# One rotation of eight PSUM banks in a sliding-window attention between two feed-forward layers: scores, maxima and sums in a new order

## The chip, the cores and the metric

The kernel runs on one core of a Trainium2 chip. A core has five engines that run side by side and wait for each other through semaphores: PE (TensorE) multiplies matrices, DVE (VectorE) and ACT (ScalarE) work on elements and can read PSUM, POOL (GpSimd) works on elements in SBUF alone, and SP (SyncE) issues DMA transfers. Results of PE land in PSUM, which has eight banks of 128 partitions by 512 fp32 values; before a bank is written again, whoever reads it has to be done. The metric is the device time of one execution in microseconds, the lower the better; the time before is the median of three runs.

## The reference

The input `x` is (8, 512, 512): eight rows of 512 tokens with 512 features. A feed-forward layer, an attention and the same feed-forward layer again are added to it:

```python
x = x + 0.5 * _L0_ffn_ref(_layernorm(x), w_gate_up, w_proj)
x = x + _L0_attn_ref(_layernorm(x), Wq, Wk, Wv, Wo)
x = x + 0.5 * _L0_ffn_ref(_layernorm(x), w_gate_up, w_proj)
```

The feed-forward layer quantises its weights to three values per group of 64, and computes `silu(gate) * up`, an RMS norm and a projection. The attention has 32 heads of 16 features and a window of 128 tokens:

```python
q, k, v = heads(x @ Wq.T), heads(x @ Wk.T), heads(x @ Wv.T)
kw, vw = ...   # each block of 128 queries sees its own and the previous block of keys
scores = jnp.einsum('bhnrd,bhncd->bhnrc', qb, kw) * scale
valid = (dist >= 0) & (dist <= window) & (key_global >= 0)
probs = jax.nn.softmax(jnp.where(valid, scores, min), axis=-1)
out = jnp.einsum('bhnrc,bhncd->bhnrd', probs, vw) ... @ Wo.T
```

## The kernel before

There are three stages: feed-forward a (`ffn_stage("a")`), attention (`attention_stage`) and feed-forward c. The change is in the attention and in the first row of stage c, which begins while the attention's last row still runs (class `FirstRow`, lines 610 to 690).

The attention is cut into 128 units: 8 rows b, in each 4 groups j of eight heads, in each 4 blocks t of 128 queries; unit u = (4b + j) * 4 + t, and i = u // 4 numbers the groups. A loop over u (line 1052) writes down the order of all engines' instructions by hand: inside `manual_schedule` (line 1041) each engine executes its instructions in the order of the program, so an instruction that waits holds up everything behind it on its engine. Waits are found by the framework: an instruction waits for the writers of what it reads, and for the last reader of a bank or buffer that it takes over.

In one step of the loop PE gets, in this order:

- `probabilities(u)` (line 917), "sp": the transposed scores of the unit, 24 matmuls of 32 rows each into four banks (three parts: two for the scores, one that adds the negated maxima `ms`). Each bank is read by a Relu: banks 0, 2 and 3 on ACT (L944), bank 1 on DVE (L940). Then ACT takes the exponential of all four (L946), and POOL clears what lies outside the window (L951, one or two instructions). The result is `pT`.
- `weighted(u - 1)` (line 957), "av": the weighted sums of the unit before, 32 matmuls (16 where t is 0) of 32 columns. Two units share one bank of the pool `ps_av`, and every second unit ACT copies it to `sums` (L977).
- `maxima(u + 6)` (line 873), "sm": the scores of the unit six steps ahead, 16 matmuls into four banks, for the maxima alone. DVE reads each bank twice (L892, eight instructions that add the window and reduce).
- every fourth unit `maxima_turned`, "neg": the maxima transposed (L911); DVE splits them in two terms just before (L902, L903).
- one projection (L808, four matmuls of 128x512), which one depends on t: at t = 0 `values` ("wv"), at t = 1 the output of an earlier row ("wo", from the second row on), at t = 2 `queries` ("wq"), at t = 3 `keys` ("wk"). Queries and keys are split into a high and a low term by `two_terms` (line 819): ACT writes the high term (L821), DVE the difference (L822); SP then moves them to `qs` and `ks` (L839, L851), which are used from three units later on. Values are copied by DVE in two halves (L864). The output is added to the residual by DVE (L1030).
- in four units of each row a transpose of the next row's normed tokens, "ptn_b" (L227), copied by ACT (L235).

The eight banks are divided: `ps_s` (line 757) has six, which the score tiles, neg and the transposes take in turn; `ps_av` and `ps_mm` have one each, for the sums and for projections. Before the first unit, steps of the loop with negative u make the first queries, keys, values and maxima. In the last row (u from 116 on) the place of the projection is taken by a chunk of stage c's first row: `row_c.chunk` (line 653), 16 matmuls into two banks, a Silu on ACT and a product on DVE; from `down_at` on, `row_c.down` makes its down projection.

Of the kernel before, what the change touches and what calls it, by code (L numbers as in the profile page):

```python
# [8 lines left out]
F32 = mybir.dt.float32  # L9
# [3 lines left out]
ALU = mybir.AluOpType  # L13
AX = mybir.AxisListType

P = 128
# [8 lines left out]
def macaron_block(  # L25
# [19 lines left out]
    nc = tc.nc  # L45
    B, T, D = x.shape
# [47 lines left out]
    PSUM = bass.MemoryType.PSUM  # L94
# [147 lines left out]
    def ffn_stage(kind, source, target, first):  # L242
# [18 lines left out]
        def banks_opened():  # L261
            for name, bufs in (("tr", 2), ("acc", 4), ("mm", 2)):
                banks[name] = pool(s, f"ps_{name}_{kind}", bufs, PSUM), name
            banks["ms"] = banks["mm"]

        def bank(use, shape, name):
            space, tag = banks[use]
            return space.tile(shape, F32, tag=tag, name=name)
# [21 lines left out]
                True, f"{kind}{b}", each=first and b == 1,  # L290
            )

        def gate_or_up(b, c, i, use="mm"):
            ps = bank(use, [P, T], f"gu_{kind}{b}_{c}_{i}")
# [315 lines left out]
        class FirstRow:  # L610
# [1 line left out]

            KEPT = 2

            def opened(self, ps_s, ps_av, ps_mm, xpool, xn, terms):
                nonlocal xnpool
                banks["mm"] = banks["acc"] = banks["tr"] = ps_s, "s"
                banks["ms"] = ps_mm, "mm"
                self.ps_av = ps_av
                xspools.append(terms)  # L620
                xpools.append(xpool)
                xnpool = xn
                self.kept, self.terms = {}, {}
                row_loaded(0)
                self.norm = norms[0]
                self.coming = []
# [9 lines left out]
            def load(self):  # L636
                if self.coming:
                    weights_loaded([self.coming.pop(0)])

            def down_opened(self):  # L640
                nonlocal hpool
                hpool = pool(s, f"h_{kind}", 3, side="right")
                xpools.append(pool(s, f"x1_{kind}", 1, side="right"))
                projection_made(pool(s, f"weights_p_{kind}", 1, side="right"))
                n = (FC - self.KEPT) // 2
                self.coming_down = [*range(n, FC // 2), *range(n)]
# [6 lines left out]
            def chunk(self, c, use):  # L653
                if c == 0:
                    self.sumsq = work.tile([P, T], F32, tag="ss", name=f"ss_{kind}0", bufs=1)
                gate = gate_or_up(0, c, 0, use)
# [15 lines left out]
            def down(self, n):  # L672
                order = [*range(FC - self.KEPT, FC), *range(FC - self.KEPT)]
                if n == 0:
                    self.ops = outputs(0)
                    banks["tr"] = self.ps_av, "av"
# [22 lines left out]

        def rest():  # L700
            xspools.append(2 * [pool(s, f"xs1_{kind}", 2)])
            banks_opened()
            for b in range(1, B):
                row(b)
            s.close()
# [20 lines left out]
    def attention_stage(row_c):  # L726
# [27 lines left out]
        fixed["wq"] = pool(asked, "wq_b", 1)  # L754

        s = ExitStack()
        ps_s = pool(s, "ps_s", 6, PSUM)
        ps_av = pool(s, "ps_av", 1, PSUM)
        ps_mm = pool(s, "ps_mm_b", 1, PSUM)

        xss, norms = {0: begun["norm"][0]}, {}

# [31 lines left out]
            nc.gpsimd.memset(tile_.bitcast(F32), 0.0)  # L794

        xrs = {}
        qs, ks, ms, pTs, avs, sums, dens_sb, reps, oTs = {}, {}, {}, {}, {}, {}, {}, {}, {}
        NJ = DC
        units = B * NJ * TB

# [1 line left out]
            return u // TB // NJ, u // TB % NJ, u % TB  # L802

        def sum_of_products(name, pairs, done):
            space, tag = (ps_mm, "mm") if 0 <= u < units else (ps_s, "s")
            ps = space.tile([P, T], F32, tag=tag, name=name)
            for n, (lhs, rhs) in enumerate(pairs):
                nc.tensor.matmul(ps, lhs, rhs, start=(n == 0), stop=(n == len(pairs) - 1))  # L808
            done(ps)
# [8 lines left out]

        def two_terms(name, ps, by):
            kept = raw.tile([P, 2, T], F32R, tag=name[0], name=name)  # L820
            nc.scalar.activation(kept[:, 0, :], ps, AF.Copy, scale=by)  # L821
            nc.vector.scalar_tensor_tensor(  # L822
                kept[:, 1, :], ps, by, kept[:, 0, :].bitcast(F32), ALU.mult, ALU.subtract
            )
            return kept

# [28 lines left out]
        def values(b, t):  # L855
            rows = slice(t * P, (t + 1) * P)
            pairs = [(xss[b][0][:, k, rows], attn_w["wv"][:, k, :]) for k in range(DC)]


            def kept(ps):  # L860
                heads = vones[b % 2][:, t].rearrange("p (j h g) d -> p h j g d", h=2, g=NG)
                made = ps.rearrange("p (j h g d) -> p h j g d", h=2, g=NG, d=DK)
                for h in range(2):
                    nc.vector.tensor_copy(heads[:, h, :, :, h::2], made[:, h])  # L864

            sum_of_products(f"wv_{b}_{t}", pairs, kept)

# [89 lines left out]
        def weighted(u):  # L957

            i, t = u // TB, u % TB
            b, j = i // NJ, i % NJ  # L960
            if t % 2 == 0:
                avs[i] = ps_av.tile([P, 2, 2, P], F32, tag="av", name=f"av_{u}")
            for h in range(2):
                blocks = [(t - 1, 1), (t, 0)] if t else [(t, 0)]
                for n, (block, m) in enumerate(blocks):
                    for g in range(NG):
                        nc.tensor.matmul(  # L967
                            avs[i][32 * g : 32 * g + 32, h, t % 2, :],
                            vones[b % 2][:, block, NG * (2 * j + h) + g, :],
                            pTs[u - t + block][:, 2 * g + h, m * P : (m + 1) * P],  # L970
                            start=(n == 0), stop=(n == len(blocks) - 1),
                        )

            if t % 2 == 1:
                if t == 1:
                    sums[i] = work.tile([P, 2, T], F32, tag="sums", name=f"sums_{i}", bufs=2)
                nc.scalar.copy(  # L977
                    sums[i][:, :, (t - 1) * P : (t + 1) * P],
                    avs.pop(i).rearrange("p h m q -> p h (m q)"),
                )  # L980

        def rows_of(t, h):

# [68 lines left out]
        for u in range(-3 * TB, down_at + FC):  # L1052
            i, t = u // TB, u % TB
            b, j = i // NJ, i % NJ
            if u == closing - row:
                row_c.opened(ps_s, ps_av, ps_mm, xpool, xnpool, [begun["xs0"], fixed["wv"]])
            if u == closing:
                first_values.close()
                row_c.working()
# [16 lines left out]
            if u == units + 1:  # L1076
                scores.close()
                row_c.weights(range(FC - 1, FC))
                row_c.load()
                row_c.down_opened()  # L1080
            if closing <= u < units:
                row_c.load()
                row_c.load()
            if 0 <= u < units:
                probabilities(u)
            if j == 3 and t == 1 and 1 < b + 3 < B:
                row_loaded(b + 3)
# [51 lines left out]
            if down_at - 3 <= u:  # L1139
                row_c.load_down()  # L1140
            if u in chunk_at:
                row_c.chunk(chunk_at[u], "mm" if u in outputs else "ms")
            if u >= down_at:
                row_c.down(u - down_at)
        row_c.ended()
# [37 lines left out]
```

## Time and profile before

| what | value |
|---|---|
| runs | 2391.74, 2395.63, 2397.71 us; median 2395.63 |
| the profiled execution | 2397.86 us, span 2396.1 us |
| busy over the span | PE 97%, weight loads 72%, DVE 55%, ACT 41%, POOL 38% |
| 0 to 803 us, stage a | PE busy 766.23 us, granted clock 0.99 |
| 803 to 847, before the first unit | PE 41.87 |
| 847 to 999, the first 24 units, most without an output projection | PE 143.94, clock 0.94 |
| 999 to 1565, 88 units, 22 groups | PE 564.50 of 566, DVE 388.37, ACT 342.59, POOL 201.76, clock 1.00 |
| 1565 to 1686, the last row with chunks of stage c | PE 112.16 of 121, clock 0.97 |
| 1686 to 1740, the last outputs and the down projection | PE 52.98 of 54 |
| 1740 to 2396, the rest of stage c | PE 646.57 of 656 |

The span is the time from the first to the last instruction; the execution's own time holds a little more. Rows of the timeline read: start in us, duration, engine, line, operation, tile written and tiles read, shapes, how many are merged, and in brackets how long the engine sat idle before and what ended that. PEld is the loading of a matmul's stationary operand, which can run under the matmul before it. Matmuls overlap each other, so the end of a merged row reaches a little into the next; the step from one start to the next start is what a block costs. Busy time on PE includes short waits inside a row of merged matmuls.

### The profile page before, as it was taken

The page shows a single profiled execution, that of the slowest core. Times are in us where ns is not written, and L with a number is a line of the kernel's source. Part 1 is how long each engine was busy: PE and PEld are TensorE (multiplying, and loading weights), DVE is VectorE, ACT ScalarE, POOL GpSimd, SP SyncE. Part 2 cuts the span into 40 slices and gives each one's busy share as a digit, 9 for nine tenths or more (in the row PEclk, how much of TensorE's full clock was granted, in tenths as well). Part 3 has the DMA queues.
Part 4 walks back from the last instruction along what each step waited for, and adds up shares of the span by engine and source line. Part 5 has one row for each costly group of instructions (what it writes and reads, how often), then busy time and mean ns, then how long its engine had stood idle before and what let it go on. Part 6 is the DMA issues. An engine that isn't in the chain of part 4 may idle for free.

```text
span 2396.1 us, 42976 instructions
## 1 busy us (share of the span) xinstructions
PE 2328.3 (97%) x16824; PEld 1718.5 (72%) x16824; DVE 1308.7 (55%) x3685; ACT 985.1 (41%) x1422; POOL 903.4 (38%) x746
## 2 busy tenths in 40 slices
PE   5999999999999999999999999999999999999998
PEld 4778888888888555555565555566688888888886
DVE  7884544444543566767667676664354444444433
ACT  6773222222222156656666656567322222222221
POOL 0000345445445223333333333335334544544544
PEclk9899999999999999999999999999999999999999
DMA  4443200100100324344444445363610010010000
GB/s 160 147 146 134 90 18 18 36 18 18 36 36 36 105 69 110 90 120 118 116 119 119 115 102 135 98 179 125 217 61 22 15 36 18 18 36 18 18 18 18
DMA packets 90283, 186.30 MB, mean 78 GB/s; under 512 B 22496, under 2 KB 26592, under 8 KB 87008
## 3 DMA queue, kind: packets, MB, share of 16 engines
q1 hardware_dynamic: 74768, 142.40, 21.1%
q10 hardware_dynamic: 15312, 41.16, 4.6%
q8 instruction: 132, 2.16, 0.4%
q14 instruction: 71, 0.58, 0.1%
HBM read 78.91 MB, written 45.88 MB: 52 GB/s over the span
## 4 chain that ended last, share of the span: by engine, by line
PE 91%; DVE 5%; ACT 2%; issue 1%; DMA 1%; POOL 0%; ACTq 0%; POOLq 0%; DVEq 0%
PE gu_c L297 19%; PE gu_a L297 18%; PE o_c L330 10%; PE o_a L330 9%; PE wv L808 5%; PE wo L808 5%; PE wq L808 5%; PE wk L808 5%; PE av L967 4%; PE sp L932 4%; PE sm L884 4%; PE neg L911 1%; PE ptn_a L227 1%; PE ptn_c L227 1%; ACT pT L946 1%
## 5 line engine op out<-in xcount | busy, mean ns | idle before, releaser
L297 PE MATMUL gu_a<-xs_a,wgu_a 128*128 128x512 f32 x2048 | 497.0, 396 | 8.0 <-ACT sg_a L308 3.0
L297 PE MATMUL gu_c<-xs_c,wgu_c 128*128 128x512 f32 x2048 | 495.1, 395 | 0.4 <-ACT sg_c L308 0.4
L297 PEld LDWEIGHTS gu_a<-xs_a,wgu_a 128*128 128x128 f32 x2048 | 385.4, 190 | 91.5 <-ACT sg_a L308 4.3
L951 POOL TENSOR_SCALAR_AFFINE_SELECT pT<-pT 128x1024 f32<-128x1024 f32 x224 | 243.7, 1108 | 533.4 <-ACT pT L946 533.4
L297 PEld LDWEIGHTS gu_c<-xs_c,wgu_c 128*128 128x128 f32 x2048 | 383.7, 189 | 84.1 <-issue 1.8
L892 DVE CUSTOM_DVE_ANT_0 seen<-sm,window 128x256 f32<-128x256 f32 (+1 forms) x1024 | 331.4, 388 | 83.9 <-PE sm L884 83.0
L330 PE MATMUL o_a<-wp_a,hs_a 128*128 128x512 f32 x1024 | 257.1, 396 | 1.5 <-DVE hs_a L322 1.4
L330 PE MATMUL o_c<-wp_c,hs_c 128*128 128x512 f32 x1024 | 254.6, 393 | 0.0
L313 DVE TENSOR_TENSOR h_c<-gu_c,sg_c 128x512 f32<-128x512 f32 x128 | 88.4, 690 | 295.1 <-PE gu_c L297 256.5
L586 POOL TENSOR_TENSOR sq_c<-h_c 128x512 f32<-128x512 f32 x120 | 125.2, 1044 | 298.6 <-DVE h_c L313 287.4
L944 ACT ACTIVATE pT<-sp 128x512 f32<-128x512 f32 x372 | 176.2, 545 | 131.2 <-PE sp L932 131.2
L330 PEld LDWEIGHTS o_a<-wp_a,hs_a 128*128 128x128 f32 x1024 | 192.9, 190 | 41.9 <-DVE hs_a L322 2.3
L330 PEld LDWEIGHTS o_c<-wp_c,hs_c 128*128 128x128 f32 x1024 | 191.9, 188 | 43.0 <-issue 1.9
L946 ACT ACTIVATE pT<-pT 128x2048 f32<-128x2048 f32 (+1 forms) x128 | 217.4, 1698 | 6.9 <-DVE pT L940 2.4
L313 DVE TENSOR_TENSOR h_a<-gu_a,sg_a 128x512 f32<-128x512 f32 x128 | 88.3, 690 | 232.4 <-PE gu_a L297 227.7
L587 POOL TENSOR_TENSOR ss_c<-ss_c,sq_c 128x512 f32<-128x512 f32 x120 | 188.4, 1570 | 9.0
L586 POOL TENSOR_TENSOR sq_a<-h_a 128x512 f32<-128x512 f32 x90 | 94.3, 1048 | 225.1 <-DVE h_a L313 215.6
L308 ACT ACTIVATE sg_c<-gu_c 128x512 f32<-128x512 f32 x128 | 76.7, 599 | 245.7 <-PE gu_c L297 236.0
L318 ACT CAST hs_c<-h_c 128x512 fp32r<-128x512 f32 x114 | 70.8, 621 | 226.1 <-DVE h_c L313 226.1
L308 ACT ACTIVATE sg_a<-gu_a 128x512 f32<-128x512 f32 x128 | 76.4, 597 | 209.0 <-PE gu_a L297 201.7
L318 ACT CAST hs_a<-h_a 128x512 fp32r<-128x512 f32 x115 | 71.3, 620 | 205.0 <-DVE h_a L313 202.6
L322 DVE TENSOR_TENSOR hs_c<-h_c,hs_c 128x512 fp32r<-128x512 f32 x114 | 111.0, 974 | 74.4 <-ACT hs_c L318 74.4
(134 smaller groups left out, 3024.5 us busy)
## 6 DMA issues: line engine op xcount, KB each, us to landing
ks<-k SPq DMA_DIRECT2D x128, 256.0 KB
qs<-q SPq DMA_DIRECT2D x128, 128.0 KB
wf_gu<-w_gate_up_dram SPq DMA_DIRECT2D x16, 512.0 KB
wgu_kept<-wgu_a ACTq DMA_DIRECT2D x16, 512.0 KB
rows_a<-x_a ACTq DMA_DIRECT2D x8, 1024.0 KB
x_b<-rows_a SPq DMA_DIRECT2D x8, 1024.0 KB
oT<-sums SPq DMA_DIRECT2D x64, 128.0 KB
rep<-inverses SPq DMA_DIRECT2D x256, 32.0 KB
```

The source lines that it names most:

```text
L297: nc.tensor.matmul(ps, wgu[c][:, i * DC + k, :], xss[b][part][:, k, :], start=(k == 0 and part == 0), stop=(k == DC - 1 and part == 1),)
L308: nc.scalar.activation(sg, gate, AF.Silu)
L313: nc.vector.tensor_tensor(h, up, sg, ALU.mult)
L318: nc.scalar.copy(hs[:, 0, :], h)
L330: nc.tensor.matmul(ops[t], hs[:, part, t * P : (t + 1) * P], wp[e // 2][:, e % 2, :], start=(e == begin and part == 0), stop=(e == end and ...
L586: nc.gpsimd.tensor_tensor(sq, h, h, ALU.mult)
L587: nc.gpsimd.tensor_tensor(sumsq, sumsq, sq, ALU.add)
L808: nc.tensor.matmul(ps, lhs, rhs, start=(n == 0), stop=(n == len(pairs) - 1))
L892: nc.vector.tensor_tensor_reduce(out=seen[:, : n * P], in0=tiles[g][:, h, : n * P], in1=window[:, (2 - n) * P :], scale=-1.0, scalar=3.4e3 ...
L944: nc.scalar.activation(under, tiles[g][:, :, : n * P], AF.Relu, scale=-1.0)
L946: nc.scalar.activation(seen, seen, AF.Exp, scale=-1.0)
L951: nc.gpsimd.affine_select(out=half, in_=half, compare_op=ALU.is_ge, fill=0.0, base=0, pattern=[[0, 2 * NG], [sign, P]], channel_multiplier ...
```

## The change

Four things, in the attention and its overlap with stage c:

1. Banks. `ps_s` gets all eight banks, and `ps_av` and `ps_mm` are gone: scores, maxima, sums, neg, projections and transposes take banks from one rotation. The sums no longer share a bank between two units: each unit has its own tile and its own copy to `sums`, with half the columns. At `down_at` the pool is closed, and stage c opens its own pools (2, 4 and 2 banks), which it did only after its first row before.
2. Order. `weighted(u - 1)` moves behind `maxima(u + 6)`, and `denominators` with it; neg, when there is one, follows the sums.
3. `two_terms`. DVE no longer subtracts ACT's term: it writes the whole scaled value (`tensor_scalar`, L822), and POOL subtracts ACT's term in place (L823). SP's transfers of the low term follow POOL.
4. `values`. The second half of the copy moves from DVE to ACT (L865).

In the changed file the lines after 822 lie a few further on: L892 becomes L893, L940 to L946 become L941 to L947, L951 becomes L952; the sums' matmuls keep L967, their copy becomes L976, the output's add L1026, and the projections' matmuls become L807.

```diff
-            def opened(self, ps_s, ps_av, ps_mm, xpool, xn, terms):
+            def opened(self, ps_s, xpool, xn, terms):
                 nonlocal xnpool
                 banks["mm"] = banks["acc"] = banks["tr"] = ps_s, "s"
-                banks["ms"] = ps_mm, "mm"
-                self.ps_av = ps_av
+                self.banks = banks
...
+            def own_banks(self):
+                banks_opened()
...
-        ps_s = pool(s, "ps_s", 6, PSUM)
-        ps_av = pool(s, "ps_av", 1, PSUM)
-        ps_mm = pool(s, "ps_mm_b", 1, PSUM)
+        own_banks = ExitStack()
+        ps_s = pool(own_banks, "ps_s", 8, PSUM)
...
         def sum_of_products(name, pairs, done):
-            space, tag = (ps_mm, "mm") if 0 <= u < units else (ps_s, "s")
+            space, tag = (ps_s, "s") if u < down_at else row_c.banks["mm"]
...
             kept = raw.tile([P, 2, T], F32R, tag=name[0], name=name)
+            whole = kept[:, 1, :].bitcast(F32)
             nc.scalar.activation(kept[:, 0, :], ps, AF.Copy, scale=by)
-            nc.vector.scalar_tensor_tensor(
-                kept[:, 1, :], ps, by, kept[:, 0, :].bitcast(F32), ALU.mult, ALU.subtract
+            nc.vector.tensor_scalar(whole, ps, by, None, ALU.mult)
+            nc.gpsimd.tensor_tensor(
+                kept[:, 1, :], whole, kept[:, 0, :].bitcast(F32), ALU.subtract
             )
...
-                for h in range(2):
-                    nc.vector.tensor_copy(heads[:, h, :, :, h::2], made[:, h])
+                nc.vector.tensor_copy(heads[:, 0, :, :, ::2], made[:, 0])
+                nc.scalar.copy(heads[:, 1, :, :, 1::2], made[:, 1])
...
-            if t % 2 == 0:
-                avs[i] = ps_av.tile([P, 2, 2, P], F32, tag="av", name=f"av_{u}")
+            av = ps_s.tile([P, 2, P], F32, tag="s", name=f"av_{u}")
...
-                            avs[i][32 * g : 32 * g + 32, h, t % 2, :],
+                            av[32 * g : 32 * g + 32, h, :],
...
-            if t % 2 == 1:
-                if t == 1:
-                    sums[i] = work.tile([P, 2, T], F32, tag="sums", name=f"sums_{i}", bufs=2)
-                nc.scalar.copy(
-                    sums[i][:, :, (t - 1) * P : (t + 1) * P],
-                    avs.pop(i).rearrange("p h m q -> p h (m q)"),
-                )
+            if t == 0:
+                sums[i] = work.tile([P, 2, T], F32, tag="sums", name=f"sums_{i}", bufs=2)
+            nc.scalar.copy(sums[i][:, :, t * P : (t + 1) * P], av)
...
+            if u == down_at:
+                own_banks.close()
+                row_c.own_banks()
...
-            if 0 <= u - 1 < units:
-                weighted(u - 1)
...
-                if t == 0:
-                    denominators(i - 1)
...
             if 0 <= u + AHEAD < units:
                 maxima(u + AHEAD)
+            if 0 <= u - 1 < units:
+                weighted(u - 1)
+            if t == 0 and 0 <= i - 1 < B * NJ:
+                denominators(i - 1)
```

The rest of the diff drops the argument `use` of `gate_or_up` and `chunk`, the list `avs`, the tag of `ps_av` in `down`, and the opening of stage c's banks in `rest`.

More of the change, by code (lines that the diff above doesn't have):

```diff
@@ L291, in row_loaded, with gate_or_up @@
             )
-        def gate_or_up(b, c, i, use="mm"):
-            ps = bank(use, [P, T], f"gu_{kind}{b}_{c}_{i}")
+        def gate_or_up(b, c, i):
+            ps = bank("mm", [P, T], f"gu_{kind}{b}_{c}_{i}")
             for k in range(DC):
@@ L651, in load_down, with chunk @@
                     nc.sync.dma_start(wp[u].bitcast(F32), wp_kept[u])
-            def chunk(self, c, use):
+            def chunk(self, c):
                 if c == 0:
                     self.sumsq = work.tile([P, T], F32, tag="ss", name=f"ss_{kind}0", bufs=1)
-                gate = gate_or_up(0, c, 0, use)
+                gate = gate_or_up(0, c, 0)
                 up = gate_or_up(0, c, 1)
@@ L675, in down @@
                     self.ops = outputs(0)
-                    banks["tr"] = self.ps_av, "av"
                 if n + 2 < FC:
@@ L701, in rest @@
             xspools.append(2 * [pool(s, f"xs1_{kind}", 2)])
-            banks_opened()
             for b in range(1, B):
@@ L796, in attention_stage @@
         xrs = {}
-        qs, ks, ms, pTs, avs, sums, dens_sb, reps, oTs = {}, {}, {}, {}, {}, {}, {}, {}, {}
+        qs, ks, ms, pTs, sums, dens_sb, reps, oTs = {}, {}, {}, {}, {}, {}, {}, {}
         NJ = DC
@@ L1055, in attention_stage @@
             if u == closing - row:
-                row_c.opened(ps_s, ps_av, ps_mm, xpool, xnpool, [begun["xs0"], fixed["wv"]])
+                row_c.opened(ps_s, xpool, xnpool, [begun["xs0"], fixed["wv"]])
             if u == closing:
@@ L1141, in attention_stage @@
             if u in chunk_at:
-                row_c.chunk(chunk_at[u], "mm" if u in outputs else "ms")
+                row_c.chunk(chunk_at[u])
             if u >= down_at:
```

## The prediction, made before the changed kernel was run

> **What bounds the kernel now.** I read the page first: the clock row (40 slices, tenths of full speed) and the chain of work that ended last, shared out by engine.
>
> ```profile
> PEclk9899999999999999999999999999999999999999
> PE 91%; DVE 5%; ACT 2%; issue 1%; DMA 1%; POOL 0%; ACTq 0%; POOLq 0%; DVEq 0%
> ```
>
> The chain is PE nearly throughout, so only PE's own order and what PE waits for can move the end; the clock is full but for the start and the end. The change lies in the attention, 803 to 1740 us. There I took the timeline between 999 and 1565 us, where 22 groups of four units follow each other almost identically; I call their units by the projection that ended the unit before. First the unit after a key projection:
>
> ```profile
> 1179.00 0.51 PE L932 MATMUL sp<-qs,ks 32*128 32x256 f32 x8
> 1179.11 0.60 ACT L821 ACTIVATE k<-wk 128x512 fp32r<-128x512 f32 x1 [3.24 <-PE wk L808]
> ...
> 1179.74 0.69 DVE L822 SCALAR_TENSOR_TENSOR k<-wk,k 128x512 fp32r<-128x512 f32 x1 [1.43 <-ACT k L821]
> 1179.91 1.08 PE L967 MATMUL av<-pT,vones_sb 128*32 128x128 f32 x32
> 1180.07 1.58 ACT L944 ACTIVATE pT<-sp 128x512 f32<-128x512 f32 x3 [0.36 <-PE sp L932]
> 1180.35 0.68 DVE L940 TENSOR_SCALAR pT<-sp 128x512 f32<-128x512 f32 x1
> 1180.92 0.90 PE L884 MATMUL sm<-ks,qs 32*128 32x256 f32 x16
> ...
> 1181.75 3.70 PE L808 MATMUL wv<-wv_sb,xs_b 128*128 128x512 f32 x8
> ```
>
> Next, the unit after a value projection:
>
> ```profile
> 1185.38 0.51 PE L932 MATMUL sp<-qs,ks 32*128 32x256 f32 x8
> 1185.49 0.76 DVE L864 COPY vones_sb<-wv 128x256 f32<-128x256 f32 x2
> ...
> 1186.29 0.64 PE L967 MATMUL av<-pT,vones_sb 128*32 128x128 f32 x16
> 1186.45 1.58 ACT L944 ACTIVATE pT<-sp 128x512 f32<-128x512 f32 x3 [2.39 <-PE sp L932]
> 1186.49 0.69 DVE L940 TENSOR_SCALAR pT<-sp 128x512 f32<-128x512 f32 x1 [0.25 <-PE sp L932]
> 1186.87 1.11 PE L884 MATMUL sm<-ks,qs 32*128 32x256 f32 x16
> 1187.91 3.70 PE L808 MATMUL wo<-wo_sb,oT 128*128 128x512 f32 x8
> ```
>
> The reader is to see that sp, av, sm and the projection start one behind the other, and that sm's length varies: 0.83 and 1.04 here, 0.67 where nothing holds it. sm's fourth tile needs the bank that L940 empties; from L940's end (1181.03, 1187.18) to the next block it is 0.72 both times. The one place where sm already follows sp directly is the first unit:
>
> ```profile
> 847.65 0.69 DVE L822 SCALAR_TENSOR_TENSOR k<-wk,k 128x512 fp32r<-128x512 f32 x1 [0.63 <-ACT k L821]
> 848.26 0.68 DVE L940 TENSOR_SCALAR pT<-sp 128x512 f32<-128x512 f32 x1
> 848.40 0.36 PEld L884 LDWEIGHTS sm<-ks,qs 32*128 32x128 f32 x2 [0.60 <-DVE k L822]
> 848.99 0.53 PEld L884 LDWEIGHTS sm<-ks,qs 32*128 32x128 f32 x13 [0.24 <-DVE pT L940]
> 849.66 0.30 PEld L808 LDWEIGHTS wv<-wv_sb,xs_b 128*128 128x128 f32 x2
> ```
>
> A released bank lets PE load 0.05 later (848.34 to 848.40, 848.94 to 848.99), and the block is over 0.67 after that. So: end of the last emptying + 0.72 = start of the next block. This row also shows sm held by a key projection's L822.
>
> **The change, part by part.** (a) Order and banks. In the changed program the fourth sm tile waits, unit after unit, for the last reader of the projection that ended just before: L822, L865 (the new half on ACT) or the output's add L1030. The sums' first matmul waits for ACT's first Relu (L944) of the same unit, whose bank it gets; the projection waits for DVE's Relu. Everything behind the waiting load in PE's queue waits too. Per unit, from sp's first matmul to the start of the projection (or of neg):
>
> After k: before 2.75. Now L822 ends at 1.43, +0.72 = 2.15, + av 1.01 = 3.16: **+0.41**.
> After v: before 2.53. L864's first half ends at 0.49, ACT's half takes about 0.39 (the 128x256 Relu) with 0.05 between: 0.93, +0.72 = 1.65. But the first Relu ends at 1186.45 + 0.60 (three take 1.58, one 0.60), that is 1.67, so av starts at 1.72; +0.58 = 2.30: **-0.23**.
> After o: before 2.58 (1191.54 to 1194.12). L1030 ends at 0.80, and sm, with half the columns, would be over by 1.45; the Relu holds av to 1.72; +1.01 = 2.73: **+0.15**.
> After q: before 2.51 (1198.11 to 1200.62). L822 ends at 1.43 again, 2.15, 3.16: **+0.65**.
>
> Sum +0.98 a group of 25.25 us. In 5 of the 22 groups a transpose (L227, 0.53) follows the projection and hides most of the emptying: L822 ends at 0.99 instead (1019.49 + 0.69 against sp at 1019.19). After o the Relu rules, 2.73 for 2.52; after q 0.99 + 0.72 + 1.01 = 2.72 for 2.51; after k the Relu, 2.73 for 2.59; after v ACT copies the transpose last, to 1.04, 2.34 for 2.53: +0.21 + 0.21 + 0.14 - 0.19 = +0.37. 17 x 0.98 + 5 x 0.37 = **18.6 us**.
>
> What would be won if no bank were late: the last four sp matmuls start 0.12 after the four before them, but av starts 0.21 after those, and sm's start costs as much again; joined, sp and sm save about 0.2 a unit, and sm's waits of 0.16 and 0.37 go. A rule of the Trainium skill stands behind this: "TensorEngine Tiling (Array Packing)", Key Properties, says that changing the tiling mode drains TensorE, and the new order changes it three times a unit instead of four. By the rule alone 128 units would save some 26 us, an estimate; the sum above goes by the rows, where the saving is spent waiting.
>
> (b) Side by side. For values ACT's half waits for DVE's half in the changed program, and for queries and keys L822 still waits for ACT's L821, though it no longer reads its output. So the bank is free no sooner: L822's 0.69 as a one-input operation is L940's 0.69. "PSUM — Partial Sum Buffer", PSUM bank collisions, speaks against the reading in parallel: two engines may not read one bank in the same partitions at once, reads included. The trace of before can't show it, as its L822 needs L821's result; taken by the rule the sum stays at +18.6, without it it is that of the first rival.
>
> (c) GpSimd's new subtraction: 64 times; bounds 1.04 (L586) and 1.57 (L587) us, I take 1.29 (L1018, two inputs of this shape). It lies off PE's path: the keys are issued at 1205.71 and the DMAs quiet down by 1217, while sm wants them at 1217.9. SP's queue shifts by 1.3 with it (dens, oT and rep behind). If that cover is gone, each group pays up to 1.3. Only at the start is it bare: sm idles 1.14 at 818.56 for the first keys, +0.9; the first unit wins 0.6 (no sums there). Net **+0.3**. The eviction of the sums in two copies of 0.39 instead of one of 0.57 costs nothing: ACT idles 2.4 to 3.2 before its next work.
>
> (d) Elsewhere. The six groups of 847 to 999 have no output projection: there the unit after v and the next took 11.5 (957.61 to 969.13), bound by sm, eight maxima on DVE and the select on POOL. Now sp of the next unit runs under the maxima: about 10.7. With +0.41 and +0.65 that is +0.3 a group; the clock was 0.94 there, and shorter idling may lift it: I take **0** (-4 to +3). Four sm stalls (0.77, 0.47, 0.78, 0.69) at 1480 to 1520 (the next row's statistics ahead of L940 on DVE) go, since the Relu now holds only the later projection: **-2.7**. Last row, 1565 to 1686: units 112 to 117 give, by the same steps, -0.50, -0.07, +0.36, +0.65, +0.41, -0.22; at 1609 sm waits for keys behind the weights' DMAs; these come 0.95 later against PE, and av's 1.01 no longer runs before that wait: +1.96; units 119 to 121 0, +0.13, -0.67. Together 2.05: **+2.0** (-4 to +6). The banks reopened for the down projection: 0, PE is 53 of 54 us busy there.
>
> Sum: 18.6 + 0.3 + 0 - 2.7 + 2.0 = 18.2. The span 2396.1 becomes 2414.3; the profiled run's 2397.86 lies 1.76 over its span and 2.23 over the median 2395.63, so the median becomes 2413.8: **2414**.
>
> **Rivals.** 1. The engines do read at the same time, so that the wait named under (b) delays nothing: L822 ends at 0.80, and after k and q the Relu rules, 2.73 and 2.53, so a plain group sums to -0.08 and one with transposes to +0.13, -0.7 in all; the early groups then win 0.8 each, -4.8, and the last row loses 1.1 less. With the start's 0.3 and the -2.7 that is -7.0: 2389, at the edge of what can be told. For it: DVE is idle 1.43 before L822. Against it: the changed program still names ACT. 7 in 100.
> 2. Faster: banks are free in time everywhere, as they would be if emptying took under 0.75 from sp's start. Then each unit is sp 0.91 (0.82 with half the columns) + sm 0.67 (0.60) + av 1.01 (0.58) less 0.2, a group 8.97 against 10.37, and 32 groups win 45 us: 2351. Against it: L821 alone ends at 0.71 and the first Relu at 1.67. It decides where av starts 1.4 after sp. 5 in 100.
> 3. Slower still: the granted clock falls with the new gaps of 0.7 in every second unit, as to 0.94 between 847 and 999: 566/0.94 - 566 = 36, so 2450; or late keys, 22 x 1.3 = 29 more, 2443. Against it: gaps of 0.8 at 1480 to 1520 left the clock at 1.00. 10 in 100.
> The forecast keeps 78 in 100.
>
> **How the numbers follow.** A difference under 0.3% (7 us) can't be told from none here. The forecast's own bounds: if the first Relu starts 0.06 earlier (847.92, 1.01 after sp, against 1.07) the steady sum falls by 2.5; if each new wait costs PE's queue another 0.05 it grows by 4.4; with the ranges above, not all at one end, 2402 to 2428; reaching towards the first and the third rival, 2398 to 2432. Slower: 0.74 of the forecast and all of the third, 0.84; same: 0.04 and half of the first, 0.08; faster: the other half and the second, 0.08.
>
> **What would show it.** Right: 26.2 us a plain group; sm's loads idle before "DVE k" and "DVE q" for some 0.6 each; av idle before "ACT pT"; L822 never starting before L821's end; clock 1.00. Wrong: sm's loads following sp without idling, L822 overlapping L821, or DMA named ahead of sm.

## The result

The changed kernel takes 2419.31 us (median of 4 runs, 2418.19 to 2421.13), the kernel before 2393.68 (4 runs, 2391.50 to 2397.71): a ratio of 1.0106, 95% interval 1.0088 to 1.0123, so 25.6 us slower by the medians. The profiled execution took 2419.16 us, with a span of 2417.4 against 2396.1; the spans are only 21.3 apart, because the profiled execution of the kernel before (2397.86) lies 4.2 above that kernel's median.

First the two lines of the page that answer to those of before, the granted clock in 40 slices and the chain of work that ended last:

```profile
PEclk9999999999999999999999999999999999999999
PE 84%; DVE 6%; ACT 4%; issue 2%; DMA 2%; POOL 1%; SPq 1%; ACTq 0%; POOLq 0%; DVEq 0%
```

The clock did not fall. PE's part of the chain fell from 91 to 84%; of the seven points ACT has two, and DVE, "issue", DMA, POOL and SP's queue one each, so the chain by itself does not say what PE waits for. Among the lines that it names there are `DVE q L822`, `DVE k L822` and `ACT pT L945`, each with 1% of the span; none of them was among the fifteen lines named before. Now the timeline of the changed kernel, the unit after a key projection (start, duration, engine, line, operation; in brackets how long the engine was idle before and what ended that):

```profile
1186.02 0.51 PE L933 MATMUL sp<-qs,ks 32*128 32x256 f32 x8
1186.12 0.60 ACT L821 ACTIVATE k<-wk 128x512 fp32r<-128x512 f32 x1 [3.23 <-DMA rep<-inverses]
...
1186.76 0.69 DVE L822 TENSOR_SCALAR k<-wk 128x512 f32<-128x512 f32 x1 [2.53 <-ACT k L821]
1186.83 0.28 PE L885 MATMUL sm<-ks,qs 32*128 32x256 f32 x3
...
1187.50 0.73 PE L885 MATMUL sm<-ks,qs 32*128 32x256 f32 x13 [0.38 <-DVE k L822]
1187.53 1.29 POOL L823 TENSOR_TENSOR k<-k 128x512 fp32r<-128x512 f32 x1 [4.13 <-DVE k L822]
...
1188.16 1.08 PE L967 MATMUL av<-pT,vones_sb 128*32 128x128 f32 x32
...
1189.17 3.70 PE L807 MATMUL wv<-wv_sb,xs_b 128*128 128x512 f32 x8
```

Three sm matmuls run, the fourth stands until DVE has read the projection's bank (1187.45), and it is 3.15 us from sp to the next projection where it was 2.75. L822 starts 0.04 after L821's end, though it no longer reads L821's output: the two engines read the bank one behind the other. So it is in the unit after a value projection too, where L865 follows L864:

```profile
1192.81 0.51 PE L933 MATMUL sp<-qs,ks 32*128 32x256 f32 x8
1192.91 0.43 DVE L864 COPY vones_sb<-wv 128x256 f32<-128x256 f32 x1 [1.08 <-PE wv L807]
...
1193.37 0.39 ACT L865 COPY vones_sb<-wv 128x256 f32<-128x256 f32 x1 [2.51 <-DVE vones_sb L864]
...
1193.87 1.57 ACT L945 ACTIVATE pT<-sp 128x512 f32<-128x512 f32 x3
...
1194.61 0.64 PE L967 MATMUL av<-pT,vones_sb 128*32 128x128 f32 x16
...
1195.18 3.70 PE L807 MATMUL wo<-wo_sb,oT 128*128 128x512 f32 x8
```

Here the first Relu (0.60 of the 1.57, so over at 1194.47) holds av until 1194.61.

The weight loads of sm and av between 999 and 1560 us show the same by sums (busy us and mean ns of one, then the idle time of PE's loads just before them and what ended it). First the kernel before, then the changed one:

```profile
L967 PEld LDWEIGHTS av<-pT,vones_sb 128*32 128x32 f32 x2448 | 61.5, 109 | 10.5
L884 PEld LDWEIGHTS sm<-ks,qs 32*128 32x128 f32 x1392 | 56.4, 183 | 20.6 <-issue 8.3 <-DVE neg_terms L902 4.4 <-DVE pT L940 3.3
```

```profile
L885 PEld LDWEIGHTS sm<-ks,qs 32*128 32x128 f32 x1347 | 60.5, 184 | 22.8 <-DVE q L822 10.0 <-DVE k L822 9.4 <-ACT xs_b L235 0.6
L967 PEld LDWEIGHTS av<-pT,vones_sb 128*32 128x32 f32 x2352 | 60.5, 109 | 20.1 <-issue 15.1
```

sm's old waits are gone (0.20 behind every av, put down to "issue" or to L902, and DVE's Relu, L940), and the projection's last reader has taken their place with 19.4 us; av has doubled its idle time. The wait for the Relu shows as "issue" on the loads, since a separate wait instruction of PE's queue holds it (the trace has 127 of these at L967, one for nearly every unit); on av's matmuls the trace names `ACT pT L945`, 7.1 us in 22 waits over the whole run.

What each unit and group costs, from start to start in the timelines, with the experiments told below (in us, the value that most units of the kind have; a plain group is one of four units without a transpose):

| kernel | after k | after v | after o | after q | plain group | units 0 to 24 | units 112 to 127 |
|---|---|---|---|---|---|---|---|
| before | 2.75 | 2.53 | 2.58 | 2.51 | 25.25 | 152.4 | 114.9 |
| after | 3.16 | 2.38 | 2.82 | 3.16 | 26.45 | 152.4 | 115.3 |
| e1, order put back | 2.60 | 2.38 | 2.58 | 2.51 | 24.95 | 156.4 | 112.1 |
| e2, banks alone | 2.59 | 2.38 | 2.58 | 2.51 | 24.96 | 148.6 | 112.3 |
| e3, order alone | 3.76 | 3.09 | 3.46 | 3.48 | 28.72 | 166.6 | 122.6 |
| e4, readers put back | 3.16 | 2.39 | 2.82 | 3.16 | 26.45 | 152.5 | 115.7 |
| e5, one reader | 2.82 | 2.39 | 2.82 | 2.52 | 25.46 | 146.9 | 114.3 |
| e6, first bank unread | 2.43 | 2.25 | 2.58 | 2.44 | 24.58 | 145.0 | 114.1 |

The four columns of units run from sp's first matmul to the projection (or to neg, after o); the last three are from a first matmul of sp to another, in the profiled execution. In the profiled execution the changed kernel stood at -0.3 us against before at the first unit, -0.4 at unit 24, +20.5 at unit 112, +20.8 at unit 127 and +21.3 at the end: nearly all of the loss is in the steady groups.

### The profile page after: what moved, and what is told of

The parts are those of the page before. It is cut to its first block, busy times and chain, and to the rows that moved or that the text cites. A ratio compares the mean times of both kernels' runs of the same rounds, so it can differ in the third digit from the quotient of the medians.

```text
span 2417.4 us, 43274 instructions
## 1 busy us (share of the span) xinstructions
PE 2321.0 (96%) x16824; PEld 1714.5 (71%) x16824; DVE 1300.8 (54%) x3653; ACT 1000.6 (41%) x1518; POOL 983.2 (41%) x810
## 3 DMA queue, kind: packets, MB, share of 16 engines
q8 instruction: 132, 2.16, 0.4%
## 4 chain that ended last, share of the span: by engine, by line
PE 84%; DVE 6%; ACT 4%; issue 2%; DMA 2%; POOL 1%; SPq 1%; ACTq 0%; POOLq 0%; DVEq 0%
PE gu_c L297 19%; PE gu_a L297 17%; PE o_c L330 9%; PE o_a L330 9%; PE wo L807 4%; PE wv L807 4%; PE wq L807 4%; PE av L967 4%; PE wk L807 3%; PE sp L933 3%; PE sm L885 3%; PE neg L912 1%; DVE q L822 1%; DVE k L822 1%; ACT pT L945 1%
## 5 line engine op out<-in xcount | busy, mean ns | idle before, releaser
L952 POOL TENSOR_SCALAR_AFFINE_SELECT pT<-pT 128x1024 f32<-128x1024 f32 x224 | 242.0, 1101 | 328.1 <-ACT pT L947 325.7
L893 DVE CUSTOM_DVE_ANT_0 seen<-sm,window 128x256 f32<-128x256 f32 (+1 forms) x1024 | 330.8, 387 | 16.7 <-PE sm L885 13.0
L947 ACT ACTIVATE pT<-pT 128x2048 f32<-128x2048 f32 (+1 forms) x128 | 217.5, 1699 | 7.1 <-DVE pT L941 3.4
L945 ACT ACTIVATE pT<-sp 128x512 f32<-128x512 f32 x372 | 176.2, 546 | 67.3 <-PE sp L933 64.5
```

The costliest lines, as they stand in the source:

```text
L893: nc.vector.tensor_tensor_reduce(out=seen[:, : n * P], in0=tiles[g][:, h, : n * P], in1=window[:, (2 - n) * P :], scale=-1.0, scalar=3.4e3 ...
L945: nc.scalar.activation(under, tiles[g][:, :, : n * P], AF.Relu, scale=-1.0)
L947: nc.scalar.activation(seen, seen, AF.Exp, scale=-1.0)
L952: nc.gpsimd.affine_select(out=half, in_=half, compare_op=ALU.is_ge, fill=0.0, base=0, pattern=[[0, 2 * NG], [sign, P]], channel_multiplier ...
```

## The experiments

All ratios are to the kernel before on the same chip.

**e1, the order put back.** In the loop of the changed kernel:

```diff
+            if 0 <= u - 1 < units:
+                weighted(u - 1)
...
             if 0 <= u + AHEAD < units:
                 maxima(u + AHEAD)
-            if 0 <= u - 1 < units:
-                weighted(u - 1)
-            if t == 0 and 0 <= i - 1 < B * NJ:
-                denominators(i - 1)
```

> The changed kernel with the order of before (scores, sums of the unit before, maxima's scores, projection); the rotation of eight banks, GpSimd's subtraction and the values' half on ACT stay. Theory (what costs time is only that the maxima's scores stand at the place where the projection's bank is not yet read, and the sums where the first Relu is not done): with the sums in between, the fourth tile of the maxima comes 2.4 us after the unit's start, later than both releases (1.48 and 1.72 us), and the old wait for DVE's Relu is gone too, so a unit is PE's own work: from the scores' start to the projection 2.59 after keys (2.75 before the change, 3.16 after it), 2.16 after values (2.53, 2.38), 2.50 after the output (2.58, 2.82), 2.50 after queries (2.51, 3.16). A plain group 24.65 us, the whole 2380 us (2373 to 2389), 14 below the kernel before. Rival A (GpSimd's step, late keys or the split readers cost the time): 2415 or more. Rival B (the rotation of eight costs by itself, order does not matter): 2405 or more.

Measured: 2385.09 us (2381.84 to 2390.38, 8 runs), ratio 0.9956 (0.9940 to 0.9973). The order alone turns the change's loss into a gain; both rivals fall. The unit after values stayed at 2.38 where 2.16 was expected: I had looked at the projection's bank only, and there the fourth sm tile still takes the bank of the unit's own first Relu.

**e2, banks alone.** e1, and the readers undone as well, so that of the change only the rotation of eight banks is left:

```diff
-        ps_s = pool(s, "ps_s", 6, PSUM)
-        ps_av = pool(s, "ps_av", 1, PSUM)
-        ps_mm = pool(s, "ps_mm_b", 1, PSUM)
+        own_banks = ExitStack()
+        ps_s = pool(own_banks, "ps_s", 8, PSUM)
```

> The kernel before with the rotation of eight banks alone; order, subtraction on DVE and values on DVE are as before. Theory: the same gain as the run with the order put back, since the readers lie off PE's path in both; 2379 us (2372 to 2389), within 3 us of that run, the difference being GpSimd's subtraction before the first maxima (0.9 us). Rival A (the new readers cost): over 8 us faster than the run with the order put back. Rival that side-by-side reading gains: over 8 us slower than it.

Measured: 2381.67 us (2380.74 to 2382.86, 6 runs), ratio 0.9940 (0.9924 to 0.9955). This version beats both kernels. Its loads in the same stretch (999 to 1560 us):

```profile
L965 PEld LDWEIGHTS av<-pT,vones_sb 128*32 128x32 f32 x2480 | 62.3, 109 | 10.6
...
L883 PEld LDWEIGHTS sm<-ks,qs 32*128 32x128 f32 x1408 | 51.2, 183 | 18.4 <-issue 8.3 <-DVE neg_terms L901 4.4 <-ACT pT L943 3.4
```

av is back at 10.6, and sm's loads are busy for 51.2 instead of 56.4 us (some of the waiting had been counted inside merged rows): DVE's Relu no longer holds them, since the tile that waited for it now takes another bank; ACT's first Relu (L943, 3.4) holds them instead, as in e1. The steps of e1 and e2 agree to 0.01 in all four columns; the 3.4 us between their medians lie in the first 24 units (156.4 against 148.6 in the profiled executions; that of e1 is 4.4 above e1's median), to which I come below.

**e3, order alone.** The kernel before, with `weighted` and `denominators` moved behind `maxima` as in the change, and its pools of 6, 1 and 1 banks kept.

> The kernel before with the new order alone: six banks in rotation, one for sums, one for projections; readers as before. Theory: the maxima's third and fourth tile now take the banks of the scores' first two tiles of the same unit, so the fourth waits for DVE's Relu; its end + 0.72 + the sums: 3.76 after keys (2.75 before), 3.10 after values (2.53), 3.46 after the output (2.58), 3.57 after queries (2.51), 3.5 us a plain group more, and the whole 2474 us (2450 to 2495), slower than the change as made. Rival (the order is good or neutral and the banks or the readers cost): 2400 us or less.

Measured: 2499.05 us (2496.32 to 2503.93, 4 runs), ratio 1.0436 (1.0411 to 1.0461). Its loads, 999 to 1560 us:

```profile
L884 PEld LDWEIGHTS sm<-ks,qs 32*128 32x128 f32 x1232 | 67.5, 183 | 64.3 <-ACT pT L944 57.6 <-DVE pT L940 6.7
L967 PEld LDWEIGHTS av<-pT,vones_sb 128*32 128x32 f32 x2144 | 54.0, 110 | 9.1
```

Three units came out to 0.01 of the worked steps (3.76, 3.09, 3.46), the unit after queries 0.09 below; 28.72 a group for 28.75. Most of the idle time goes to ACT's first Relu (57.6 us), because the third sm tile stands before the fourth in PE's queue and waits for that one; the fourth then waits the rest for DVE's Relu, which ends last and sets the step. The total is above its range of 2450 to 2495, because the first 24 units and the last row also took 14 and 8 us more than before. The new order needs many banks at once: with six for scores and maxima it costs 102 us, with eight in rotation 25.

**e4, the readers put back.** The changed kernel, with `scalar_tensor_tensor` on DVE again (no GpSimd step) and both halves of the values on DVE.

> The changed kernel with both readers undone: DVE subtracts again (no GpSimd step), values are copied by DVE alone; order and eight banks stay. Theory: the two engines were never side by side, so the banks are free as late as before: 2418 us (2414 to 2422), no difference. Rival A (GpSimd's step and later keys cost): 2410 us or less. Rival C (reading by two engines does gain something): 2424 us or more.

Measured: 2419.01 us (2416.62 to 2420.80, 6 runs), ratio 1.0094 (1.0078 to 1.0111): no difference from the change as made, and no column of steps differs by more than 0.01. Reading by two engines neither won nor cost anything in this order, and 64 subtractions on GpSimd lie off the path.

**e5, one reader.** In the changed kernel, queries and keys:

```diff
-            nc.scalar.activation(kept[:, 0, :], ps, AF.Copy, scale=by)
-            nc.vector.tensor_scalar(whole, ps, by, None, ALU.mult)
+            nc.scalar.activation(whole, ps, AF.Copy, scale=by)
+            nc.vector.tensor_copy(kept[:, 0, :], whole)
```

> The changed kernel, but queries and keys are read from PSUM once: ACT writes the whole scaled value (0.60 us), DVE makes the high term from SBUF, GpSimd subtracts as in the change. Theory: the projection's bank is free at 0.75 instead of 1.48 us after the unit's start, so the maxima's scores follow without waiting and only the first Relu holds the sums: 2.82 us from the scores' start to the projection after keys (3.16 in the changed kernel), 2.50 after queries (3.16), values and output as they were; 1.0 us less a plain group, 2398 us (2390 to 2406). The maxima's loads name no DVE k or q any more, the sums' idle before ACT pT grows. Rival (the wait for the projection's reader only hides the same wait for the Relu, so nothing is won): 2415 us or more.

Measured: 2395.17 us (2392.31 to 2398.58, 12 runs), ratio 0.9995 (0.9984 to 1.0006). 24 of the 25.6 us lost are back with two lines, and the order still stands. What is left of the waits, 999 to 1560 us:

```profile
L967 PEld LDWEIGHTS av<-pT,vones_sb 128*32 128x32 f32 x2432 | 63.6, 109 | 29.0 <-issue 28.4
L885 PEld LDWEIGHTS sm<-ks,qs 32*128 32x128 f32 x1392 | 56.7, 184 | 2.7 <-ACT xs_b L235 0.8
```

sm's idle time falls from 22.8 to 2.7 us and av's grows from 20.1 to 29.0: of the 20.1 us that sm no longer waits, av now waits 8.9, for the Relu.

**e6, the first bank unread.** e5, and:

```diff
-                    nc.scalar.activation(under, tiles[g][:, :, : n * P], AF.Relu, scale=-1.0)
+                    nc.scalar.activation(under, tiles[g or 2][:, :, : n * P], AF.Relu, scale=-1.0)
```

> The changed kernel with queries and keys read once, and with the first Relu of each unit reading the third score tile instead of the first: the first tile's bank has no reader, and a quarter of the probabilities is computed from the wrong scores (what is left out is the reading of that bank; every engine has as many instructions as before). Theory (the two late banks are all that keeps the new order from winning): the sums' first matmul follows the maxima's scores at once, so from the scores' start to the projection 2.49 us after keys (2.82 with one reader alone), 2.05 after values (2.38), 2.40 after the output (2.82), 2.40 after queries (2.52); 1.2 us a plain group less than with one reader alone, 2366 us (2356 to 2376), which is also below the kernel with banks alone (2.59, 2.38, 2.58 and 2.51 there). Rival (the next bank is as late: DVE's Relu holds the projection, or the order saves nothing even with free banks): 2381 us or more.

Measured: 2375.84 us (2374.99 to 2376.32, 4 runs), ratio 0.9914 (0.9891 to 0.9938), at the upper end of the range. With both banks free the order does win, also against e2's (24.58 a group for 24.96), but by 5.8 us where the expectation has 15.7; the two ratios' intervals overlap a little, while the steps of the units do not. The unit after queries, timeline:

```profile
1260.17 0.44 PE L933 MATMUL sp<-qs,ks 32*128 32x128 f32 x8
...
1260.90 0.77 PE L885 MATMUL sm<-ks,qs 32*128 32x256 f32 x16
1260.91 1.07 DVE L822 CAST q<-q 128x512 fp32r<-128x512 f32 x1 [2.86 <-ACT q L821]
...
1261.60 1.08 PE L967 MATMUL av<-pT,vones_sb 128*32 128x128 f32 x32
...
1262.61 3.70 PE L807 MATMUL wk<-xs_b,wk_sb 128*128 128x512 f32 x8
```

sp, sm and av follow each other without a wait. In two other units the next wait was already there: after values sm's fourth tile waits for the values' two readers (av starts 1.67 after sp, as L865's end + 0.72 gives), and after the output neg starts 0.11 after DVE's second `neg_terms` (L904), which comes behind DVE's Relu, 0.13 later than av alone would let it; that it is L904 that holds it I read from the order of these ends, no run took it away.

**e7, sums in pairs.** e2, with one bank for the sums of two units again:

```diff
-            av = ps_s.tile([P, 2, P], F32, tag="s", name=f"av_{u}")
+            if u == 0 or t % 2 == 1:
+                avs[0] = ps_s.tile([P, 2, 2, P], F32, tag="s", name=f"av_{u}")
+            av = avs[0][:, :, t % 2, :]
```

> Banks alone (order and readers of before, rotation of eight), and the sums of two units share one bank again, now the units with odd and the following even t, each copied by ACT at once. Theory: in the unit after values the fourth tile of the maxima no longer takes the bank of the scores' first tile but the projection's, released 0.5 us earlier than it is wanted; that unit becomes 2.16 us instead of 2.38, the others stay, 27 groups save 6 us: 2376 us (2371 to 2380). Rival (what ends at 2.38 there is PE's own work, or another bank is as late): 2382 us, no difference from banks alone.

Measured: 2381.60 us (2380.50 to 2385.01, 6 runs), ratio 0.9941 (0.9924 to 0.9958): no difference from e2, and outside the 2371 to 2380 that I expected. The unit after values:

```profile
1255.53 1.57 ACT L943 ACTIVATE pT<-sp 128x512 f32<-128x512 f32 x3 [2.44 <-PE sp L931]
...
1255.95 0.96 PE L883 MATMUL sm<-ks,qs 32*128 32x256 f32 x16
1256.84 0.30 PEld L807 LDWEIGHTS wo<-wo_sb,oT 128*128 128x128 f32 x2
```

The first Relu ends at 1256.13, and 0.71 later wo is there: the wait that was to go is still there. By these times the fourth sm tile was given the bank of the unit's first score tile in this program too; I had counted tiles to find which bank comes next, and with one of them kept for two units that gave the wrong bank. So the run says nothing on what that unit would take without its wait.

**e8, early groups.** e2, with ACT's exponential moved behind the copy of the sums, and in the first 24 units the sums at t = 2 behind the query projection:

```diff
+            late = t == 2 and 0 < u < closing and u - 1 not in outputs
-            if 0 <= u - 1 < units:
+            if 0 <= u - 1 < units and not late:
                 weighted(u - 1)
+            if 0 <= u < units:
+                powers(u)
...
                 queries(i + 3)
+            if late:
+                weighted(u - 1)
```

> Banks alone, and two steps moved: ACT's exponential comes behind the copy of the sums (so that their bank is free some 2 us earlier), and in the groups without an output projection the sums at t = 2 come behind the query projection, which then covers their wait for GpSimd's select. Theory: in the six groups up to 999 us, where the sums wait 1.9 us for the select and the scores for the sums' bank, a group of 24 to 27 us loses 1 to 3 us; later groups stay as they are: 2373 us (2362 to 2380). Rival (these groups are held by DVE's maxima or GpSimd, whatever PE's order): 2381 us or more.

Measured: 2395.32 us (2392.86 to 2398.60, 12 runs), ratio 0.9994 (0.9982 to 1.0005): 14 us slower than e2, all of it in those 24 units (163.1 us for 148.6). The run moves two things at once, and what the later exponential does alone was not tried. The timeline of one such unit (its scores begin at 963.3), and below it the query projection of e2:

```profile
966.43 1.11 PE L883 MATMUL sm<-ks,qs 32*128 32x128 f32 x13 [0.36 <-DVE negs L891]
...
968.56 1.08 PE L910 MATMUL neg<-ident,neg_terms 128*128 128x128 f32 x4 [1.02 <-DVE neg_terms L902]
...
969.44 5.26 PE L807 MATMUL wq<-xs_b,wq_sb 128*128 128x512 f32 x8
...
970.30 0.34 PEld L807 LDWEIGHTS wq<-xs_b,wq_sb 128*128 128x128 f32 x1 [0.52 <-issue]
...
974.63 1.08 PE L969 MATMUL av<-pT,vones_sb 128*32 128x128 f32 x32
```

```profile
959.59 3.60 PE L807 MATMUL wq<-xs_b,wq_sb 128*128 128x512 f32 x8
```

sm and neg wait for DVE's maxima and terms, so the sums had stood at a place where PE was idle anyway; moved behind the projection they cost their 1.01, 6.1 us in six groups. And the projection itself now takes 5.26 for 3.60: the six query projections take 10.0 us more than six undisturbed ones, in e2 1.7 more. 6.1 + 8.3 is 14.4 of the 14.5 us. The time is the rival's, and in the unit shown PE waits for DVE even with the sums out of the way; how much of that is DVE's own work and how much GpSimd's slowing of it (last section) was not separated.

## Why the prediction was right

**The mechanism (a).** It forecast 2414 (2398 to 2432; measured 2419.31) and that the loss lies in the waits of sm's fourth tile for the projection's last reader and of av for the first Relu. The step after keys was forecast as 3.16 and is 3.16, after queries 3.16 and 3.16. e1 and e2 show that the order makes the loss (put back, it is a gain), e5 and e6 that within the order it is these two banks: the first one freed gives back what was worked out for it (e5: 2.82 for 2.82, 2.52 for 2.50), and with both free the order is a gain. The rival of two engines reading at once is excluded by the rows (L822 0.04 behind L821, L865 0.03 behind L864), "late keys" by e4 and "the clock falls" by the clock row.

**What was mis-sized.** The step "after v: -0.23" measured -0.15, "after o: +0.15" measured +0.25. Both are units where av waits for the Relu, and I had let av start 0.05 after its end, as a released bank lets a load start; its first load starts 0.11 after, its first matmul 0.14. After o the step from neg to the projection has also grown by 0.03 (0.49 for 0.46). So a plain group loses 1.20 instead of 0.98, 3.7 us over 17 groups, and one with transposes 0.70 instead of 0.37, 1.7 over five. Together that is 5.4, most of it seen in the 4.9 us by which the steady part (20.8) exceeds the forecast's 18.6 - 2.7. (The sum 17 x 0.98 + 5 x 0.37 is 18.5, not the 18.6 that I wrote; the forecast loses 0.1 us by it.)

**(b), side by side.** Right: L822 never begins before L821's end, L865 not before L864's, and e4 shows that the reading by two engines is worth nothing here. That L822 needs no result of L821 any more did not matter: the changed program makes the second reader of a bank wait for the first. "PSUM — Partial Sum Buffer", PSUM bank collisions, in the Trainium skill gives a reason for such a wait, that two engines on one bank in the same partitions collide; whether the chip would stand two readers at once was not tried, so no run here shows it.

**The rule on switching.** The forecast set "TensorEngine Tiling (Array Packing)" in the Trainium skill, Key Properties, that a change of the tiling mode drains TensorE, against the rows: by the rule alone a gain of some 26 us, with 0.2 a unit taken from the rows for each switch saved. With no bank late the order of e6 saves 0.16 after keys and 0.07 after queries against e2 (2.43 for 2.59, 2.44 for 2.51). So a saved switch agrees with the rule in sign, but in these two units it is worth 0.07 to 0.16, not 0.2; that it is a drain which takes this time no run shows by itself. Against that the projection's late bank costs 0.34 after keys and 0.64 after queries (the changed kernel against e5).

**(c), GpSimd's subtraction.** Nothing in the steady part, as forecast (e4: no column of steps differs by over 0.01). Before the first unit I had put +0.3; it was -0.3. Between e1 and e2, which differ only in the readers, there are 3.4 us in the medians, all in the first 24 units of the profiles. GpSimd's step may cost something there, but about 3.9 of the 7.8 us by which the two profiles differ in these units are query projections that ran slowly (last section), in the changed order e4 and the changed kernel, with the same difference in readers, have 152.5 and 152.4, and the intervals of the two ratios overlap: it was not settled.

**(d), elsewhere.** The six early groups were forecast at 0 and gave -0.1 (152.4 both times), as the sum of single units that went from -3.1 to +1.2. That they cancel so well is luck: part of these steps comes from query projections that ran slowly in one of the two profiles. The four stalls at 1480 to 1520 us were forecast to save 2.7: the eight units from 99 on differ by -0.3 where two plain groups would lose 2.4, so 2.7. The last row was forecast at +2.0 and gave +0.8, but not by its largest term. At 1609 us I had sm wait for keys, at +1.96; the rows of before have sm wait there for DVE's Relu (L940, 0.27 on its matmuls) and neg for DVE's terms (L903, 1.61), no DMA is named, and that unit took 10.98 for 10.86, +0.12. Units 112 to 117 gave +0.88 for the forecast's +0.63, and the smaller differences after unit 118 made up the rest.

**The sum.** 18.2 was forecast for the span, 21.3 measured; 3.1 of the 5.5 us between 2413.8 and 2419.31 are that. It is so little by luck in part: the steady groups were forecast 4.9 too low, the start, the early groups and the last row 1.9 too high. The other 2.4 are the median's place: I took the profiled execution of before as 2.23 above the median, and that of the changed kernel is at its median.

**Faster than both.** The second rival, banks free in time everywhere, was priced at 2351. It was not what the change does. With those two banks free the kernel takes 2376 us (e6), since neg and the values' readers are next; and the units that waited for nothing took 2.43 after keys and 2.44 after queries where the rival's terms give 2.39 and 2.30, so its price was too low as well. What pays is the part of the change that I had not priced by itself: eight banks in one rotation under the old order (e2, 2382 us) remove DVE's Relu from sm's way, 2.75 to 2.59 and 2.53 to 2.38.

## What to carry to other kernels

When two blocks of PE's work are moved together, count the banks that are open at that moment: the projection being read, four scores being read and four maxima being written are nine, and whoever comes ninth waits for the reader of the bank that it is given. Do not stop at the number of banks: take each bank's last reader's end from the rows of the profile, and look whether the order before had put other work exactly where the readers needed time. A bank that is read once and finished in SBUF was free earlier here than one read by two engines in turn (e5).

## What the runs showed of the hardware

**PE's rate after idling.** A query projection takes 3.60 us, but in the early groups, where PE waits for DVE, some take 4.6 to 5.6: in e8 all six (4.83 to 5.56), in e1 three of six at 4.9 to 5.3 and two at 4.1, in e2 one at 5.17, in the kernel before one at 5.22. Its weight loads are then 0.85 or 0.86 us apart instead of 0.43, half the rate, and the granted clock over the 25 us around it is 0.86 (e1, 846 to 871 us; e8, 948 to 973) where it is 1.00 in undisturbed stretches. In the e8 unit above, taken in short stretches, it is 1.00 until 965.5, 0.50 from 966 to 972.5 and 1.00 again from 973. "TensorE: Matmul & The Clock Gate" in the Trainium skill, Part 1, says that the array's clock is halved when it has been idle for a while. The halving agrees with these rows; how long a wait it takes they do not show, since the clock fell at 966 among gaps of 0.4 us, and before PE's longest gap there, the 1.02 ahead of neg. So in these groups a wait of PE was paid for again in the projection behind it. The gaps of 0.4 to 0.7 us in the steady groups left the clock at 1.00 in the changed kernel; in e3, with longer ones, it was 0.99 (1012 to 1656 us).

**DVE beside GpSimd.** A tiny operation of DVE in SBUF, 0.17 us, takes four to six times as long in rows where GpSimd works beside it. In the changed kernel:

```profile
857.03 2.13 POOL L952 TENSOR_SCALAR_AFFINE_SELECT pT<-pT 128x1024 f32<-128x1024 f32 x2 [2.41 <-ACT pT L947]
857.47 0.69 DVE L903 CAST neg_terms<-negs 128x16 fp32r<-128x16 f32 x1
858.20 1.01 DVE L904 TENSOR_TENSOR neg_terms<-negs,neg_terms 128x16 fp32r<-128x16 f32 x1
859.13 0.17 DVE L903 CAST neg_terms<-negs 128x16 fp32r<-128x16 f32 x1
859.33 0.19 DVE L904 TENSOR_TENSOR neg_terms<-negs,neg_terms 128x16 fp32r<-128x16 f32 x1
```

L904 ends 0.05 after GpSimd's two selects do (859.16), and the same two operations take 0.17 and 0.19 after that. The copy of e5 from SBUF to SBUF took 0.43 for keys and 0.74 for queries, which fall together with GpSimd's product (L1014, 1273.59 to 1274.87, the copy from 1274.41 to 1275.15). So in these rows work given to GpSimd was not free for DVE where both work in SBUF; no run took those operations of GpSimd away to prove it. DVE's reads of PSUM at L822 kept their length, 0.69 in all 64 of the changed kernel.
